# The last eight heads of the last batch divided tile by tile on chip, and finished rows stored through GpSimd's queue, in a two-layer state-space, attention and expert kernel

## The chip, the cores and the metric

The kernel runs on one core of one Trainium2 chip. The metric is the device time of the whole program in microseconds (us), taken as the median of several runs. Beside these runs there is one profiled execution, whose trace gives the durations of single instructions. All data are 32-bit floats.

## The reference

Two layers run over x of 8 x 512 rows of 256 columns. Layer 0 adds a state-space block and a top-1 expert block to x; layer 1 adds an attention block and a capacity-limited top-2 expert block. The change touches the end of layer 1 alone:

```python
xn = _layernorm(x, axis=-1)
x = x + attention(xn) + experts(xn)

q = xn @ Wq
latent_kv = (xn @ Wk + xn @ Wv) @ W_down_kv
k, v = latent_kv @ W_up_k, latent_kv @ W_up_v
scores = clip(einsum('bhqd,bhkd->bhqk', q, k) / 16)
scores = clip(scores * decay)
attn = softmax(scores, axis=-1)
out = einsum('bhqk,bhkd->bhqd', attn, v)
return out.transpose(0, 2, 1, 3).reshape(B, S, 256) @ Wo
```

There are 8 batches (b), 16 heads of 16 columns, and 512 queries and keys per batch. The softmax's division by the row sum may stand after the product with v, since the sum belongs to a query row and a head: this is what the kernel does. Each row's sum comes out of the same product, because v carries a 17th column of ones per head.

## The kernel before, in words

**Layer 1's attention.** The 16 heads of a batch are handled four at a time (group g = 0 to 3), and the 512 query rows 128 at a time (tile c = 0 to 3). One (b, g, c) is a step; there are N = 128 steps, in that order. A step has a first part (`scores`, L1370): TensorE makes `s_ps`, 128 queries by 512 keys for each of four heads; VectorE clamps it (L1382), multiplies it by the decay band and takes the row's maximum (L1384), and negates the maximum (`ng`, L1388). ScalarE then takes the exponentials (L1392). TensorE turns them (`p_ps`, L1399: four 128x128 transposes per head), ScalarE copies them out (`pT`, L1400), and TensorE multiplies with v (`values`, L1408) into `o_ps`: 32 rows per head (16 columns of v, the sum in row 16, and unused rows), four heads one above the other, 512 queries along the columns. The product is made for two tiles c at a time, columns 0 to 255 after c = 1 and 256 to 511 after c = 3.

**Dividing.** When a group's `o_ps` is full, `divide` (L1414) copies it to `os` (ScalarE, L1418) and stores it in DRAM scratch `od` (L1419). After an odd group, eight heads are read back (L1429), laid out as `oT`: head by head 16 rows, so that 128 partitions hold half of the 256 output columns. The sums come back as `sm`, 128x32 (L1430). VectorE takes the reciprocal (L1435), this goes to scratch `rd` (L1436) and comes back broadcast to 16 rows a head as `rb` (L1438); VectorE multiplies (L1441). These pieces are separated by `yield`s: in each step of the loop every waiting chain is taken one piece further. After group 3, `finish` (L1337) multiplies the turned heads with Wo (`fin`, L1341), copies this out (`fo`, L1343) and adds it to the batch's rows of `x_sb` (L1345), one tile of 128 rows at a time.

**The experts' part.** Expert outputs are added row by row into `x1` in DRAM by GpSimd's indirect DMAs (L1267). When the last one has landed, `combine` (L1354) issues on GpSimd's queue one DMA of 512 KB per batch that adds `x1`'s rows into `x_sb` (L1357). When a batch has both been added and finished, `send` (L1351) stores its 512 KB to the output from SyncE's queue (L1352).

**What sets the order.** This part is written in an order made by hand (`manual_schedule`): the program's order is every engine's order, and SyncE, GpSimd and the compute engines each work through their own list, with waits on semaphores. The loop runs over n = 0 to N + 2. In pass n it issues the scores of step n, a piece of each chain, the exponentials of step n - 1, and the transposes of step m = n - 2; when m is even, the product with v for steps m - 2 and m - 1 comes ahead of the transposes. `fill` puts pieces of the experts' work, the next batch's projections and `finish` between them; `more` takes `combine` further. After the loop the remaining chains are emptied. In SyncE's list the six stores of batches 0 to 5 stand between the two scratch stores L1419 of batch 6's groups 2 and 3.

Of the kernel before, what the change touches and what calls it, by code (L numbers as in the profile page):

```python
# [9 lines left out]
FP = mybir.dt.float32  # L10
I32 = mybir.dt.int32
AF = mybir.ActivationFunctionType
ALU = mybir.AluOpType
# [4 lines left out]
P = 128  # L18
B, S, DM = 8, 512, 256
NT = B * S  # L20
NTILE = NT // P
TPB = S // P
KC = DM // P
# [20 lines left out]
AH, AD, DL = 16, 16, 64  # L44
# [9 lines left out]
def bc(ap, axis, shape):  # L54

    return ap.unsqueeze(axis).to_broadcast(shape)
# [3 lines left out]
def tile_kernel(ctx: ExitStack, tc: tile.TileContext, t, out: bass.AP):  # L60
    nc = tc.nc
    V, A, G, T, Y = nc.vector, nc.scalar, nc.gpsimd, nc.tensor, nc.sync
# [13 lines left out]
    ident = ctile("ident", [P, P])  # L76
# [38 lines left out]
    def rows_of(src, b):  # L115
        return src[b * S : (b + 1) * S, :].rearrange("(c p) d -> p c d", p=P)
# [199 lines left out]
    for d in range(2):  # L316
        for q in range(2):
            r = slice(q * HP2, (q + 1) * HP2)
# [171 lines left out]
    with ExitStack() as es:  # L490
        p1, p2, psum = m1, m2, mp
# [22 lines left out]
        held = {}  # L514
# [206 lines left out]
        class Batch:  # L721
            def __init__(self, b):
                self.b = b
# [279 lines left out]
        N = len(chunk)  # L1003
# [35 lines left out]
        with tc.manual_schedule(engines=ENGINES):  # L1039
# [32 lines left out]
            rows, rest = itertools.chain(route0(), blocks()), late()  # L1072

            def fill(n):
                for _ in range(n):
                    if next(rows, "end") == "end":
                        next(rest, None)
# [69 lines left out]
    x_sb = res.tile([P, NTILE, DM], FP, name="x_sb", tag="x_sb")  # L1147
    with tc.tile_pool(name="a1", bufs=1) as p1, tc.tile_pool(name="a2", bufs=2) as p2, tc.tile_pool(
        name="ap", bufs=1, space=PSUM
# [139 lines left out]
        def load_some(k):  # L1289
            for to, of in loads[:k]:  # L1290
                Y.dma_start(out=to, in_=of)
            del loads[:k]
# [38 lines left out]
        def turn(pool, i):  # L1331
# [2 lines left out]
            V.tensor_copy(at, slot1[:, i, :])  # L1334
            return at

        def finish(b, oT):  # L1337
            for c in range(TPB):
                fp = bank("fin", [P, DM])
                for j in range(KC):  # L1340
                    T.matmul(fp, oT[:, j, c * P : (c + 1) * P], w_o[:, j, :], start=(j == 0), stop=(j == KC - 1))  # L1341
                fo = p2.tile([P, DM], FP, name="fo", tag="fo")
                A.copy(fo, fp)  # L1343
                xi = x_sb[:, b * TPB + c, :]
                V.tensor_tensor(xi, xi, fo, ALU.add)  # L1345
                yield
            finished.add(b)
            if b in combined:
                send(b)

        def send(b):  # L1351
            Y.dma_start(out=rows_of(out, b), in_=x_sb[:, b * TPB : (b + 1) * TPB, :])  # L1352

        def combine():  # L1354

            for b in range(B):
                G.dma_start(out=x_sb[:, b * TPB : (b + 1) * TPB, :], in_=rows_of(x1, b), accum_op=ALU.add)  # L1357
                combined.add(b)
                if b in finished:
                    send(b)  # L1360
                yield

# [49 lines left out]
        def divide(b, g, op, od, rd, held):  # L1414


            os = p1.tile([P, S], FP, name="os", tag="row", bufs=2)
            A.copy(os, op)  # L1418
            Y.dma_start(out=od[g].rearrange("i r s -> (i r) s"), in_=os)  # L1419
            yield  # L1420
            if g % 2 == 0:
                return
            j = g // 2
            if j == 0:
                held.append(p1.tile([P, KC, S], FP, name="oT", tag="oT"))
            oT = held[0]
            sm = p2.tile([P, 32], FP, name="sm", tag="sm")
            for gg in range(2):
                Y.dma_start(out=oT[64 * gg : 64 * gg + 64, j, :], in_=od[2 * j + gg, :, :AD, :])  # L1429
                Y.dma_start(  # L1430
                    out=sm[64 * gg : 64 * gg + 64, :],
                    in_=od[2 * j + gg, :, AD, :].rearrange("i (p f) -> i p f", f=32),
                )
            yield
            V.reciprocal(sm, sm)  # L1435
            Y.dma_start(out=rd[8 * j : 8 * j + 8, :].rearrange("h (p f) -> (h p) f", f=32), in_=sm)  # L1436
            rb = p1.tile([P, S], FP, name="rb", tag="row", bufs=2)
            Y.dma_start(out=rb, in_=bc(rd[8 * j : 8 * j + 8, :], 1, [8, AD, S]))  # L1438
            yield
            yield  # L1440
            V.tensor_tensor(oT[:, j, :], oT[:, j, :], rb, ALU.mult)  # L1441
            yield
            if g == 3:
                urgent.insert(0, finish(b, oT))
# [4 lines left out]
        with tc.manual_schedule(engines=ENGINES):  # L1449
# [3 lines left out]
            finished, combined = set(), set()  # L1453
            urgent, idle, chains = [], [], []
# [30 lines left out]
            def follow():  # L1485

                nonlocal work, ready, e1, e2
                if late_left:
                    last_rows(LATE[n])
                    return  # L1490
                if next(routing, "end") != "end":
                    return
                for _ in range(2):
                    if next(sends, "end") == "end" and ready is None:
                        ready = n
                        r1s.close()
                        e1 = es.enter_context(tc.tile_pool(name="f1", bufs=1, side="right"))
                        e2 = es.enter_context(tc.tile_pool(name="f2", bufs=2, side="right"))
                        work = experts()
                        next(work)  # L1500

            steps = [(b, g, c) for b in range(B) for g in range(4) for c in range(TPB)]
            N = len(steps)
            last_rows(1)
            done = []
            pT, op, pair = {}, {}, None
            inputs = {0: got}
            for n in range(N + 3):

                if n < N:  # L1510
                    b, g, c = steps[n]
                    if (g, c) == (0, 3) and b + 1 < B:
                        xT = p2.tile([P, KC, S], FP, name="xT", tag="xT")
                        Y.dma_start(out=xT, in_=xtd1[b + 1])
                    if (g, c) == (1, 2) and b + 1 < B:
                        inputs[b + 1] = {"q": [], "k": []}
                        urgent.append(inputs_of(b + 1, xT, inputs[b + 1]))
                    if (g, c) == (0, 0):
                        od = dram.tile([4, 4, 32, S], FP, name="od", tag="od", bufs=2)
                        rd = dram.tile([AH, S], FP, name="rd", tag="rd", bufs=2)  # L1520
                        scratch = (od, rd, [])
                    now = Step(b, g, c, inputs[b])
                    now.scratch = scratch
                    done.append(now)
                    now.scores()
                load_some(6)
                for chain in list(chains):
                    if next(chain, "end") == "end":
                        chains.remove(chain)
                if ready is not None and n == ready + 3:  # L1530
                    idle.append(work)
                begun = n >= 1
                if begun:
                    fill()
                if 1 <= n <= N:
                    done[n - 1].exps((0, 1))
                m = n - 2
                if m >= 0 and m % 2 == 0 and m >= 2:

                    s = done[m - 1]  # L1540
                    if s.c == 1:
                        s_op = psum.tile([P, S], FP, name="o_ps", tag="o_ps", bufs=1)
                    s.values(s_pT, s_op)
                    if s.c == TPB - 1:
                        chains.append(divide(s.b, s.g, s_op, *s.scratch))
                        next(chains[-1])
                    if begun:
                        fill()
                if 0 <= m < N:
                    if m % 2 == 0:  # L1550
                        s_pT = [p2.tile([P, TPB, 2 * P], FP, name="pT", tag="pT", bufs=5) for _ in range(4)]
                    done[m].transpose(s_pT, (0, 1))
                if begun:
                    fill() or more()
                if 1 <= n <= N:
                    done[n - 1].exps((2,))
                if 0 <= m < N:
                    done[m].transpose(s_pT, (2,))
                    if m % 2 == 1 and n < N // 2:
                        fill()  # L1560
                    done[m].transpose(s_pT, (3,))
                if begun:
                    fill() or more()
                if 1 <= n <= N:
                    done[n - 1].exps((3,))
                follow()
            while fill() or chains:
                for chain in list(chains):
                    if next(chain, "end") == "end":
                        chains.remove(chain)  # L1570
# [76 lines left out]
```

## Time and profile before

| what | value |
|---|---|
| median of the runs | 2120.34 us (three runs, 2119.49 to 2121.51) |
| the profiled execution's own time | 2089.04 us |
| its span, first to last instruction | 2087.3 us |
| mean granted TensorE clock | 0.940 of full speed |
| TensorE matmuls busy | 1838.5 us (88%) |
| VectorE busy | 1434.2 us (69%) |
| ScalarE busy | 1176.7 us (56%) |
| GpSimd busy | 624.6 us (30%) |
| SyncE's DMA queue (q1) | 116,400 packets, 137.07 MB, 20.9% of 16 engines |
| GpSimd's DMA queue (q0) | 27,504 packets, 107.25 MB, 16.8% of 16 engines |

The busy shares are means over the whole program, which has very different stages; they do not tell what the end of it waits for. For this the trace is read by place. The chain that ended last goes back from the last instruction, at each step to what released it. The timeline of one engine lists its instructions in order: start, duration, the instruction with the tiles that it writes and reads, how many of the kind were merged into the line, and in brackets the idle time ahead of it with what ended it. "SPq" lines are DMA issues on SyncE's queue; a merged line's duration reaches from its first issue to the end of its last. The windows view gives for a stretch its length, each engine's busy time with the number of instructions (TensorE, weight loads, VectorE, ScalarE, GpSimd), the granted TensorE clock, the DMA engines' busy share and GB/s. In the trace a transpose leaves one TensorE record and a matmul with data in 32 bits two, so that a `fin` tile, which is two matmuls, shows as x4.

### The profile page before, as it was taken

The numbers are of one execution on the slowest core, as the hardware profiler recorded it, in microseconds if no ns is written. First come the engines' busy times: TensorE is split into PE (matmuls) and PEld (weight loads), VectorE is DVE, ScalarE is ACT, GpSimd is POOL, SyncE is SP. The second block draws the span as 40 slices with busy tenths as digits, with TensorE's granted clock in tenths as the row PEclk, the third lists the DMA queues.
The fourth block names the chain that finished last, engine by engine and source line by source line (L and its number), as shares of the span: only waits on it lengthen the run. The fifth ranks groups of instructions, "written<-read, shape, count | busy, mean of one in ns | idle before, by whom it ended". The sixth has DMA issues, their size and how long they took to land. (4 is left out here: it accounts for less than half of the span.)

```text
span 2087.3 us, 33144 instructions
## 1 busy us (share of the span) xinstructions
PE 1838.5 (88%) x11672; PEld 1219.8 (58%) x11672; DVE 1434.2 (69%) x3299; ACT 1176.7 (56%) x2545; POOL 624.6 (30%) x565
## 2 busy tenths in 40 slices
PE   5666999999999999978776888999999999999875
PEld 5333776676677676744544445656656566665543
DVE  5684757666486756678657898766666777777783
ACT  2243454535444453545434677767677777777864
POOL 0048645446464544545420065000100000010200
PEclk9887999999999999998876889999999999999988
DMA  7113654655465565444433142231322223221711
GB/s 262 61 51 115 224 191 160 206 176 196 147 198 185 163 202 180 144 139 126 152 111 101 61 151 67 82 106 46 84 83 63 73 66 97 60 84 59 151 48 37
DMA packets 153542, 256.10 MB, mean 123 GB/s; under 512 B 23737, under 2 KB 111980, under 8 KB 141472
## 3 DMA queue, kind: packets, MB, share of 16 engines
q1 hardware_dynamic: 116400, 137.07, 20.9%
q0 software_dynamic: 27504, 107.25, 16.8%
q10 hardware_dynamic: 9472, 9.67, 1.4%
q8 instruction: 92, 1.51, 0.3%
q14 instruction: 74, 0.61, 0.1%
HBM read 185.28 MB, written 73.63 MB: 124 GB/s over the span
## 5 line engine op out<-in xcount | busy, mean ns | idle before, releaser
L1382 DVE TENSOR_SCALAR s<-s_ps 128x512 f32<-128x512 f32 x512 | 317.6, 682 | 199.9 <-PE s_ps L1377 156.4
L1392 ACT ACTIVATE s<-s,ng 128x512 f32<-128x512 f32 x512 | 355.2, 727 | 37.6 <-DVE ng L1388 37.4
L1399 PE MATMUL p_ps<-ident,s 128*128 128x128 f32 x2048 | 286.1, 283 | 48.8 <-ACT pT L1400 48.8
L1384 DVE CUSTOM_DVE_ANT_0 s<-s,band 128x512 f32<-128x512 f32 x512 | 322.9, 686 | 0.0
L1399 PEld LDWEIGHTS p_ps<-ident,s 128*128 128x128 f32 x2048 | 236.5, 144 | 128.3 <-ACT pT L1400 86.0
L1400 ACT COPY pT<-p_ps 128x512 f32<-128x512 f32 x512 | 276.6, 590 | 54.6 <-PE p_ps L1399 50.8
L1267 POOL DMA_INDIRECT x<-e_yo,e_to x28 | 44.6, 1592 | 601.1 <-ACT e_yo L1266 540.5
L732 PE MATMUL pj<-xT,w_in 128*128 128x512 f32 x384 | 204.1, 658 | 16.2 <-DVE cv L745 14.2
L1377 PE MATMUL s_ps<-kT,qT 16*128 16x512 f32 x1024 | 164.0, 671 | 27.5 <-DVE s L1382 21.0
L544 PEld LDWEIGHTS h_ps<-xdT,w 128*128 128x128 f32 x1248 | 150.1, 194 | 21.4 <-issue 20.8
L544 PE MATMUL h_ps<-xdT,w 128*128 128x128 f32 x1248 | 153.8, 277 | 1.9 <-DMA w<-in_w_dram,w_idx 1.9
L745 DVE SCALAR_TENSOR_TENSOR cv<-pj,w_conv_w,cv 128x511 f32<-128x511 f32 (+2 forms) x192 | 143.1, 746 | 10.9 <-ACT cv L741 6.9
L562 PE MATMUL y_ps<-w,hT 128*128 128x256 f32 x624 | 150.0, 385 | 0.0
L908 POOL TENSOR_TENSOR au<-da,half 128x512 f32<-128x512 f32 x64 | 76.9, 1202 | 223.0 <-PE seg L924 121.1
L562 PEld LDWEIGHTS y_ps<-w,hT 128*128 128x128 f32 x624 | 118.3, 194 | 32.5 <-issue 17.9
L1408 PE MATMUL o_ps<-pT,vt 128*32 128x256 f32 x2048 | 136.8, 408 | 0.0
L732 PEld LDWEIGHTS pj<-xT,w_in 128*128 128x128 f32 x384 | 72.6, 207 | 101.1 <-issue 93.1
L982 POOL TENSOR_TENSOR yT<-yT,ex 128x512 f32<-128x512 f32 (+1 forms) x48 | 59.1, 1231 | 221.5 <-DVE ex L981 163.4
L1248 PE MATMUL e_hp<-e_xdT,e_w 128*128 128x256 f32 x448 | 121.8, 394 | 3.1 <-ACT e_xdT L1233 2.3
L1261 PE MATMUL e_yp<-e_w,e_hT 128*128 128x256 f32 x448 | 120.1, 391 | 0.2
L937 ACT ACTIVATE mt<-seg,mid 64x64 f32<-64x64 f32 x512 | 109.5, 309 | 0.8
L1408 PEld LDWEIGHTS o_ps<-pT,vt 128*32 128x32 f32 x2048 | 64.0, 116 | 75.4 <-issue 45.2
(278 smaller groups left out, 3008.6 us busy)
## 6 DMA issues: line engine op xcount, KB each, us to landing
ex<-exd SPq DMA_DIRECT2D x96, 128.0 KB
u<-in_u_dram SPq DMA_DIRECT2D x16, 512.0 KB
xtd<-xT SPq DMA_DIRECT2D x16, 512.0 KB
fr<-fdd SPq DMA_DIRECT2D x64, 128.0 KB
od<-os SPq DMA_DIRECT2D x32, 256.0 KB
xT<-xtd SPq DMA_DIRECT2D x15, 512.0 KB
e_w<-in_ei_dram SPq DMA_DIRECT2D x7, 1024.0 KB
e_w<-in_eo_dram SPq DMA_DIRECT2D x7, 1024.0 KB
```

Of the source, the lines that this page charges most:

```text
L544: T.matmul(hp[:, i, :], w1[:, k * FF + f * P : k * FF + (f + 1) * P], xdT[:, k * P : (k + 1) * P], start=(k == 0), stop=(k == KC - 1),)
L562: T.matmul(yp, hT[f // 4][:, f % 4, :], w2[:, f * DM : (f + 1) * DM], start=(f == 0), stop=(f == FC - 1))
L732: T.matmul(pj, w_in[:, k, o * P : (o + 1) * P], self.xT[:, k, :], start=(k == 0), stop=(k == KC - 1))
L745: V.scalar_tensor_tensor(cv[:, s:], pj[:, : S - s], conv_w[:, q, 3 - s : 4 - s], cv[:, s:], ALU.mult, ALU.add)
L1248: T.matmul(hp, w1[:, k, f * P : (f + 1) * P], xdT[:, k, :], start=(k == 0), stop=(k == KC - 1))
L1377: T.matmul(sp[i], self.q[r, cols], self.k[r, :], start=True, stop=True)
L1382: V.tensor_scalar(self.p[i], sp[i], -CLAMP, CLAMP, ALU.max, ALU.min)
L1384: V.tensor_tensor_reduce(out=self.p[i], in0=self.p[i], in1=band[:, at : at + S], scale=1.0, scalar=-3.0e38, op0=ALU.mult, op1=ALU.max, acc ...
L1392: A.activation(self.p[i], self.p[i], AF.Exp, bias=self.ng[:, i : i + 1])
L1399: T.transpose(pp[:, k, :], self.p[i][:, k * P : (k + 1) * P], ident)
L1400: A.copy(pT[i][:, :, cc * P : (cc + 1) * P], pp)
L1408: T.matmul(op[32 * i : 32 * i + 32, half * 2 * P : (half + 1) * 2 * P], self.v[:, k, h * (AD + 1) : h * (AD + 1) + 32], pT[i][:, k, :], st ...
```

## The change

It has two parts.

**The last eight heads.** In batch 7, group 2's `os` is kept on chip and not stored. For group 3, `divide` is not used. A new class `Ending` handles one tile of 128 query rows: `out` copies the tile's 128 columns of `o_ps` to `osq` (ScalarE); `divide` turns group 2's and group 3's 128x128 pieces (two transposes into `tq`), so that queries are on the partitions and each head's sum is a column, takes the reciprocal of the eight sums (128x8) and multiplies (VectorE, into `oq`, 128x128); `back` turns the result (`tb`) and ScalarE copies it into `oT`; `project` multiplies with Wo (`finq`), adds to `x_sb` straight out of PSUM, and stores the tile's 128 KB from SyncE. For tiles 0 and 1 `out` and `divide` stand at the end of pass n = N, and `back` in pass N + 1 ahead of the transposes of step 127. After the loop come, in this order, `out` of tiles 2 and 3, `project` of tiles 0 and 1, and `divide`, `back` and `project` of tiles 2 and 3.

**The stores.** `send` issues on GpSimd's queue instead of SyncE's, and `combine` issues all eight loads in one piece and the stores of the finished batches in the next. In the instruction order GpSimd's list ends with eight loads and then seven stores (batches 0 to 6); SyncE's list has no 512 KB store left, and ends with four of 128 KB.

```diff
@@ -1334,6 +1334,40 @@
             V.tensor_copy(at, slot1[:, i, :])
             return at
 
+        class Ending:
+            def __init__(self, b, c, op, held):
+                self.i, self.c, self.op, (self.oT, self.os) = b * TPB + c, c, op, held
+                self.at = slice(c * P, (c + 1) * P)
+
+            def out(self):
+                self.last = p2.tile([P, P], FP, name="osq", tag="osq")
+                A.copy(self.last, self.op[:, self.at])
+
+            def divide(self):
+                tq = psum.tile([P, 2, P], FP, name="tq", tag="s_ps", bufs=4)
+                T.transpose(tq[:, 0, :], self.os[:, self.at], ident)
+                T.transpose(tq[:, 1, :], self.last, ident)
+                tq = tq.rearrange("p g (i r) -> p (g i) r", r=32)
+                sm = p2.tile([P, 8], FP, name="smq", tag="smq")
+                V.reciprocal(sm, tq[:, :, AD])
+                self.oq = p2.tile([P, 8, AD], FP, name="oq", tag="oq")
+                V.tensor_tensor(self.oq, tq[:, :, :AD], bc(sm, 2, [P, 8, AD]), ALU.mult)
+
+            def back(self):
+                tp = psum.tile([P, P], FP, name="tb", tag="s_ps", bufs=4)
+                T.transpose(tp, self.oq.rearrange("p h d -> p (h d)"), ident)
+                A.copy(self.oT[:, 1, self.at], tp)
+
+            def project(self):
+                fp = psum.tile([P, DM], FP, name="finq", tag="s_ps", bufs=4)
+                for j in range(KC):
+                    T.matmul(fp, self.oT[:, j, self.at], w_o[:, j, :], start=(j == 0), stop=(j == KC - 1))
+                V.tensor_tensor(x_sb[:, self.i, :], x_sb[:, self.i, :], fp, ALU.add)
+                Y.dma_start(out=out[self.i * P : (self.i + 1) * P, :], in_=x_sb[:, self.i, :])
+
         def finish(b, oT):
             for c in range(TPB):
                 fp = bank("fin", [P, DM])
@@ -1349,16 +1383,16 @@
                 send(b)
 
         def send(b):
-            Y.dma_start(out=rows_of(out, b), in_=x_sb[:, b * TPB : (b + 1) * TPB, :])
+            G.dma_start(out=rows_of(out, b), in_=x_sb[:, b * TPB : (b + 1) * TPB, :])
 
         def combine():
 
             for b in range(B):
                 G.dma_start(out=x_sb[:, b * TPB : (b + 1) * TPB, :], in_=rows_of(x1, b), accum_op=ALU.add)
                 combined.add(b)
-                if b in finished:
-                    send(b)
-                yield
+            yield
+            for b in finished:
+                send(b)
 
 
 
@@ -1416,6 +1450,9 @@
 
             os = p1.tile([P, S], FP, name="os", tag="row", bufs=2)
             A.copy(os, op)
+            if b == B - 1 and g == 2:
+                held.append(os)
+                return
             Y.dma_start(out=od[g].rearrange("i r s -> (i r) s"), in_=os)
             yield
             if g % 2 == 0:
@@ -1503,7 +1540,7 @@
             N = len(steps)
             last_rows(1)
             done = []
-            pT, op, pair = {}, {}, None
+            tails = []
             inputs = {0: got}
             for n in range(N + 3):
 
@@ -1524,6 +1561,9 @@
                     done.append(now)
                     now.scores()
                 load_some(6)
+                if n == N + 1:
+                    for one in tails:
+                        one.back()
                 for chain in list(chains):
                     if next(chain, "end") == "end":
                         chains.remove(chain)
@@ -1541,9 +1581,11 @@
                     if s.c == 1:
                         s_op = psum.tile([P, S], FP, name="o_ps", tag="o_ps", bufs=1)
                     s.values(s_pT, s_op)
-                    if s.c == TPB - 1:
+                    if m > N - TPB:
+                        tails += [Ending(s.b, c, s_op, s.scratch[2]) for c in (s.c - 1, s.c)]
+                    elif s.c == TPB - 1:
                         chains.append(divide(s.b, s.g, s_op, *s.scratch))
-                        next(chains[-1])
+                        next(chains[-1], None)
                     if begun:
                         fill()
                 if 0 <= m < N:
@@ -1564,6 +1606,20 @@
                 if 1 <= n <= N:
                     done[n - 1].exps((3,))
                 follow()
+                if n == N:
+                    for one in tails:
+                        one.out()
+                    for one in tails:
+                        one.divide()
+            for _ in rows:
+                pass
+            for one in tails[2:]:
+                one.out()
+            for one in tails[:2]:
+                one.project()
+            for part in ("divide", "back", "project"):
+                for one in tails[2:]:
+                    getattr(one, part)()
             while fill() or chains:
                 for chain in list(chains):
                     if next(chain, "end") == "end":
```

## The prediction

> **What bounds the kernel now.** Times are us from the span's start. I read first the chain that ended last, then the timelines of SyncE's queue and of VectorE where the chain leaves the engines for a DMA, then the stretches' clock and DMA share. Up to 1973 the chain runs through TensorE, ScalarE and VectorE, and VectorE repeats a step of one row tile every 5.05 us (its clamps start at 1963.17, 1968.21, 1973.26). It leaves the engines twice: for `od<-os` at 1975.95, and for everything after 2061.4.
>
> First place. SyncE's queue:
>
> ```profile
> 1955.99 19.87 SPq L1352 DMA_DIRECT2D out_dram<-x_sb  x6
> 1975.95 0.54 SPq L1419 DMA_DIRECT2D od<-os  x1
> ...
> 1986.39 0.51 SPq L1429 DMA_DIRECT2D oT<-od  x1
> 1986.94 0.51 SPq L1430 DMA_DIRECT2D sm<-od  x1
> ```
>
> and VectorE:
>
> ```profile
> 1978.22 0.17 DVE L1388 TENSOR_SCALAR ng<-mx 128x4 f32<-128x4 f32 x1
> 1990.53 0.35 DVE L1435 RECIPROCAL sm<-sm 128x32 f32<-128x32 f32 x1 [12.14 <-DMA sm<-od]
> 1990.80 2.42 DVE L1382 TENSOR_SCALAR s<-s_ps 128x512 f32<-128x512 f32 x4
> ```
>
> Six stores (batches 0 to 5), each waiting for its accumulating load to land, hold SyncE for 20 us. `os` was copied by 1965.09 (ACT L1418), but its store to scratch leaves at 1975.95, 10.9 us late, and lands 10.37 us later by the chain, where the same transfer takes 1.99 us on idle queues (2062.01). The reciprocal of the sums stands in VectorE's order at 1978.4, waits 12.14 us, and all scores wait behind it. The stretches:
>
> ```profile
> 1972.00:1980.00 8.00, 6.53 (x68) 3.81 (x64) 6.32 (x18) 7.01 (x13) 0.00 (x0) 1.00 1.18 239
> 1984.00:1988.00 4.00, 0.00 (x0) 0.00 (x0) 0.00 (x0) 0.00 (x0) 0.00 (x0) 0.63 0.25 86
> 1992.00:1996.00 4.00, 4.00 (x16) 1.89 (x18) 3.96 (x13) 0.10 (x1) 0.00 (x0) 0.50 0.18 66
> ```
>
> The DMA engines are full (share 1.18) from 1952 to about 1983; then all engines are empty, and TensorE comes back at clock 0.50.
>
> Second place, the tail, in the chain:
>
> ```profile
> 2058.77 2.60 PE o_ps L1408 x32
> 2062.01 1.99 DMA od<-os
> 2064.62 3.96 DMA sm<-od
> 2069.06 1.41 DMA rd<-sm
> 2070.49 3.44 DMA rb<-rd
> 2074.05 0.70 DVE oT L1441
> 2074.80 1.24 PE fin L1341 x2
> 2076.48 2.09 PE fin L1341 x4
> 2079.01 1.92 PE fin L1341 x4
> 2081.38 1.15 PE fin L1341 x4
> ```
>
> From the end of `o_ps` (2061.36) to the span's end (2087.3) are 25.9 us: a trip through DRAM to divide (12.7 to 2074.05), the multiply, projections of 8.6 us at half clock, a store of 512 KB from 2083.41 (3.9).
>
> [...]`od<-os`, in SyncE's ring behind stores, took 10.37 us. [...] Trace: last matmul at 1981.4, 0.63 in 1984 to 1988, then 0.50; eight `s_ps` take 3.86 us instead of 1.14. [...]
>
> **The change, part by part.** The sum is made against the profiled execution, 2089.04 us with a span of 2087.3; the runs' median is 2120.34, 31.3 above it, and I carry the difference in us over to it.
>
> *Stores on GpSimd.* Seven stores of 512 KB leave SyncE and stand behind the eight loads on GpSimd. Each waits there for its own load, the seventh also for VectorE's last `fin` add of batch 6. Behind them GpSimd has nothing, and only the program's end waits for them. Loads cost GpSimd 10.39 us for eight to issue, 1.3 each; I price a store the same and, as they hang on landings, up to 11.1 (the loads' median to landing): 7 x 11.1 = 78 from 1960 gives 2038, ahead of the end. Cost nothing; cover gone if a store takes 14 us.
>
> *The stall.* SyncE now issues `od<-os` at about 1965.1. The loads landed 3.1 to 3.2 us apart until stores mixed in (1955.99, 1959.10, 1962.30) and 4.4 afterwards, so all eight last until about 1956 + 7 x 3.15 = 1978; the stores follow them in one ring. The scratch store has only GpSimd's ring against it: with equal turns its 1.99 us become 3 to 4, landing at 1969. The two DMAs after it (`oT`, `sm`) and landing took 4.1 us at 1986.39; contended I take 6: 1975, 3 us before the reciprocal's place. So the 12.14 us go. Bounds: none left, or, if equal turns do not hold and the 10.37 stays, sums at 1965.1 + 10.4 + 6 = 1981.5, 3 us left; if also `sm` crawls, 6. What is late next: `rd` and `rb` (1.41 + 3.44, issued at 1978.8) have until the multiply two steps later, 10.1 us; doubled, they are in time. With no idle TensorE stays warm, and the 0.95 us that VectorE then waited for `s_ps` (before 2002.49) goes: **-13.1**.
>
> *Scratch for the last eight heads.* For g = 2 of batch 7 `os` is only held: one DMA less, hidden, 0. For g = 3 the copy of 128x512 and the whole trip go (below).
>
> *The block between steps 126 and 127.* It stands in ScalarE's order after the last exponential and before the four `pT` copies of step 127, and in TensorE's before its 16 transposes, so both wait in it, and `o_ps` and all of the ending wait for them. Now:
>
> ```profile
> 2056.35 0.75 ACT L1392 ACTIVATE s<-s,ng 128x512 f32<-128x512 f32 x1
> 2056.98 1.09 ACT L1400 COPY pT<-p_ps 128x512 f32<-128x512 f32 x2
> 2058.32 1.07 ACT L1400 COPY pT<-p_ps 128x512 f32<-128x512 f32 x2 [0.26 <-PE p_ps L1399]
> ```
>
> New prices: a 128x128 copy on ScalarE is, along 128x256 (0.37) and 128x512 (0.58), 0.27[...]; VectorE's 128x128 multiply, along 0.42 and 0.69, 0.29[...]; the reciprocal of 128x8 lies between 0.17 (128x4) and 0.35 (128x32), taken 0.2; a transpose is 0.14 in a row and 0.28 alone; the hop between engines is 0.04 to 0.06. Strided PSUM reads aren't in the trace[...]. First `osq` 2056.98 to 2057.25, transpose to 2057.6, reciprocal and multiply to 2058.2, the second tile's to 2058.75, second `tb` to 2059.1. The transposes of step 127 start at 2058.95 instead of 2056.05; from there ScalarE needs 0.65 to the first copy and 0.48 for each next: last `pT` done at 2062.05 instead of 2059.39. `o_ps` ends 1.97 later as before: 2064.05. **+2.7**; with doubled reads +4, at least +2.
>
> *The ending.* From the end of `o_ps`: two `finq` tiles of the finished columns (warm 1.03 each) 2.1; four transposes to 2.65 (their `osq` copies are done at 0.6); VectorE, after its second add (2.5), reciprocals and multiplies to 3.05 and 3.6; `tb` to 3.95; `oT` copies to 4.25; `finq` of the last two from 3.8 to 4.85 and 5.85; add to 6.35; SyncE's store. Four stores of 128 KB replace one of 512; three are under way earlier. The last is priced at `od<-os`'s 1.99 (256 KB), bounds 1.5 and 3.9. Sum 8.4 instead of 25.9: **-17.5**.
>
> *Clock.* The block leaves TensorE mostly waiting for about 2 us. At half clock `o_ps` costs 3.5 instead of 1.93 (seen at 2029.6) and each `finq` 1 more: 2.5 to 4 on the path. I allow **+1.4**.
>
> Sum: -13.1 + 2.7 - 17.5 + 1.4 = -26.5; the profiled execution would become 2062.5, the median 2093.8. Its own range: -29 (no clock loss, short store) to -19 (6 us of stall left, doubled reads), 2091 to 2101.
>
> **Rivals.** *A: the DMA engines stay the bound (0.17).* The stall came from full engines, not from the queue's order: GpSimd's ring holds loads and stores until about 1989, and the sums still land at 1985 to 1990. For: share 1.18, and no bytes go. Against: [...]the loads' own pace. Saving 26.5 less 7 to 13: 2101 to 2107.
>
> *B: the block and a cold TensorE eat half of the tail (0.10).* Strided reads at double price (+1.5), half clock from `o_ps` to the last `finq` (+4), last store 3.9 (+2): saving 19, 2101. Against: clock 1.00 from 2036 to 2064.
>
> *C: slower (0.02).* GpSimd's stores end the program. [...] If every store takes over 18 us, seven from 1960 end after 2087, and from there each us per store costs 7; at 20 us, 2133 in the median. Against: eight loads issued at 1.3 us beside a full VectorE.
>
> *D: nothing moves (0.02).* In the instruction orders of the two kernels the stores do leave SyncE and VectorE's tail is new, so only an equal loss could hide it: 2120.
>
> **How the numbers follow.** The forecast has 0.69, A 0.17, B 0.10, C 0.02, D 0.02. Range 2090 to 2106: it leaves out a little on both sides. A measurement of this kernel tells about 0.2% (4 us) from no change. Faster is the forecast with A and B, 0.96; same D, 0.02; slower C, 0.02.
>
> **What would show it.** VectorE waits under 1 us for batch 6's second reciprocal of sums, and TensorE's clock stays 1.0 there; `od<-os` at about 1965 lands within 4 us. TensorE starts step 127's transposes about 3 us after those of step 126 end. From the end of `o_ps` to the span's end 8 to 10 us; span about 2061. GpSimd's last store leaves well before. Wrong if the sums still land after 1981, or if one of the new small operations takes over 0.6 us.

## The result, and the profile after

The changed kernel takes 2100.49 us (median of seven runs, 2097.25 to 2113.6) against 2120.55 before (seven runs): ratio 0.990, interval [0.987, 0.993], 20 us less by the medians. The forecast was 2093.8, range 2090 to 2106: right in sign and range, and 7 us too good.

The profiled execution after took 2100.49 us (span 2098.8), but the one shown of before took 2089.04, 31 us under its own runs. That gap arises upstream, around 1200 to 1340 us, where GpSimd's sends of rows (L1315) wait for one line of VectorE (L1322) 50 us in the trace of after and 20 in that of before. The change is not what makes it: e5, the changed kernel on another chip, has 23.5 there. What does make it stays open. So traces are compared here by place, from the start of GpSimd's first accumulating load, which I call zero: 1949.52 before, 1979.51 after.

**The stall.** The chain of waits of after, and VectorE's timeline:

```profile
1997.92 0.59 ACT os L1452
...
1998.53 9.22 DMA od<-os
...
2008.34 7.26 DMA sm<-od
```

```profile
2015.72 0.35 DVE L1472 RECIPROCAL sm<-sm 128x32 f32<-128x32 f32 x1 [4.07 <-DMA sm<-od]
```

The stores are no longer ahead of `od<-os`: it leaves when `os` is copied (1998.5). Yet it takes 9.22 us, barely less than the 10.37 of before, and `sm` 7.26. VectorE's wait fell from 12.14 to 4.07 and did not go.

**GpSimd** carries the stores, at 0.75 us each from the third on (its timeline):

```profile
1979.51 10.46 POOL L1391 DMA_DIRECT2D x_sb<-x  x8 [2.59 <-DMA x<-e_yo,e_to]
...
2000.94 0.75 POOL L1386 DMA_DIRECT2D out_dram<-x_sb  x1 [1.90 <-DMA x_sb<-x]
2041.43 0.75 POOL L1386 DMA_DIRECT2D out_dram<-x_sb  x1 [39.74 <-issue]
```

**The ending**, from the chain:

```profile
2081.80 0.17 ACT osq L1347
...
2082.97 0.91 PE tb L1361 x2
2083.88 3.11 PE p_ps L1433 x16
2086.99 2.62 PE o_ps L1442 x32
2089.61 1.94 PE finq L1367 x8
...
2093.26 1.74 PE finq L1367 x8
```

There is no DMA left in it but the last store: 9.2 us from the end of `o_ps` to the span's end (25.9 before). No new operation is dear. The block's `osq` and `tb` stand ahead of step 127's transposes, as forecast.

**The clock** of after, in stretches (TensorE's granted clock is the third number from the end):

```profile
1988.00:1992.00 4.00, 2.10 (x14) 1.70 (x12) 4.00 (x10) 3.36 (x7) 3.50 (x4) 0.86 1.23 188
1992.00:1996.00 4.00, 4.00 (x30) 1.39 (x32) 2.76 (x8) 2.51 (x5) 1.10 (x2) 0.50 1.23 195
2016.00:2020.00 4.00, 3.33 (x8) 1.37 (x8) 4.00 (x10) 0.18 (x1) 0.00 (x0) 0.77 0.17 52
```

TensorE ran at half clock from about 1990.9 to 1997.7 with work before it; just ahead, up to 1990.56, was a gap of 1.90 us in that work. The reciprocal's place came 3.2 us later after zero than before; that the half clock did this is likely and not shown apart, but in e5, without half clock there, the place is where it was before.

### The profile page after: what moved, and what is told of

The parts are those of the page before. It is cut to its first block, busy times and chain, and to the rows that moved or that the text cites. A ratio compares the mean times of both kernels' runs of the same rounds, so it can differ in the third digit from the quotient of the medians.

```text
span 2098.8 us, 33158 instructions
## 1 busy us (share of the span) xinstructions
PE 1857.0 (88%) x11684; PEld 1227.0 (58%) x11684; DVE 1433.7 (68%) x3305; ACT 1178.8 (56%) x2548; POOL 629.1 (30%) x572
## 5 line engine op out<-in xcount | busy, mean ns | idle before, releaser
L1433 PE MATMUL p_ps<-ident,s 128*128 128x128 f32 x2048 | 296.8, 289 | 57.8 <-ACT pT L1434 49.8
L1433 PEld LDWEIGHTS p_ps<-ident,s 128*128 128x128 f32 x2048 | 245.3, 148 | 141.5 <-ACT pT L1434 84.8
L1411 PE MATMUL s_ps<-kT,qT 16*128 16x512 f32 x1024 | 167.3, 685 | 19.1 <-DVE s L1416 12.4
L544 PEld LDWEIGHTS h_ps<-xdT,w 128*128 128x128 f32 x1248 | 149.2, 192 | 22.4 <-issue 21.6
```

What stands on the lines that cost most here:

```text
L544: T.matmul(hp[:, i, :], w1[:, k * FF + f * P : k * FF + (f + 1) * P], xdT[:, k * P : (k + 1) * P], start=(k == 0), stop=(k == KC - 1),)
L1411: T.matmul(sp[i], self.q[r, cols], self.k[r, :], start=True, stop=True)
L1433: T.transpose(pp[:, k, :], self.p[i][:, k * P : (k + 1) * P], ident)
```

## The experiments

Theory: the gain is the sum of two separate parts, the ending and the order in SyncE's queue; what is left of the stall comes from GpSimd's own transfers, loads that hold back `od` and stores that hold back `sm`. Rivals: the ending gives all; the DMA engines' bytes decide, not the order; SyncE's sequencer is late. e1 to e4 ran on one chip, e5 to e8 on a second, e9 to e11 on a third, each set beside runs of the kernel before, whose medians were 2087.2 to 2087.9 us.

**e1, the kernel before once more** (no edit).

> The kernel before, unchanged, profiled once more. Why: its first profiled execution took 2089 us where its runs take 2119 to 2134, and GpSimd's eight loads began 30 us earlier in it (1949.5 us) than in the changed kernel's (1979.5). If that gap is the program's own slow or quick passage through the row-sending stage, as I think, the loads begin at about 1980 here, the execution takes about 2120, and from the first load to the end of the span it is again about 138 us, with VectorE's wait for sm at 10 to 14 us. The rival, that the change itself delays the loads by 30 us: they begin at 1950 again and the execution takes 2090.

Measured: 2088.65 us, loads from 1948.6, wait 12.43 us, 138.3 from zero to the span's end. My guess on the 31 us fell: on the chips of these experiments the kernel's medians lie near 2087, and 2120 belongs to the first timing; whether to its chip or its occasion was not tried. The rival falls too: e5 shows no delay of the loads by the change. Single profiles of the experiments start their loads anywhere from 1942 to 1952 (e8, which holds them back, apart), so stretches are counted from zero.

**e2, the new ending alone.** From the changed kernel:

```diff
 def send(b):
-    G.dma_start(out=rows_of(out, b), in_=...)
+    Y.dma_start(out=rows_of(out, b), in_=...)
...
     combined.add(b)
-yield
-for b in finished:
-    send(b)
+    if b in finished:
+        send(b)
+    yield
```

> The new ending alone (tile by tile, divided by columns and turned back); the six finished batches' stores stay on SyncE's queue as before the change. My theory, that the two halves are separate sums: 13 us less than before (about 2107), with VectorE's wait for sm still near 12 us and 17 to 18 us from the last exponential to the end of the span. Rival one, the ending gives all of it: 20 us less (about 2100). Rival two, the ending takes effect only when the queue is cleared: 5 us less or none.

Measured: 2069.76 against 2087.16, ratio 0.992 [0.990, 0.993], 17.4 us less, between my 13 and the first rival's 20. VectorE still waits 12.1 us for `sm`; from the last exponential to the span's end 17.3 us instead of e1's 32.2. The ending's gain is its own, and by place it is 15; the profile's loads also began 3 us earlier than e1's.

**e3, the stores' move alone** (the kernel before, with the edits of e2 the other way and batch 7's store left on SyncE).

> The stores' move alone: the old ending, with the last batch's own store left on SyncE so that the end is the same; batches 0 to 6 are stored through GpSimd's queue behind the eight loads. My theory: VectorE's wait for sm falls from 12 us to about 4, the stretch from the last exponential to the end stays near 31 us, and the whole is 5 to 8 us less than before (2112 to 2115). Rival, the stores' move is worth all that I forecast for it: 13 us less (2107). Rival two, it is worth nothing, since the DMA engines carry the same bytes: 2119 to 2121.

Measured: 2078.83, ratio 0.996 [0.994, 0.997], 8.3 us less; the stretch from the last exponential to the end stays at 31.0. Waits of VectorE from the first load on, e3:

```profile
DVE sm L1435 <- DMA sm<-od: 21.8, 2, 16.3
```

Two waits, the longer one (16.3) in the old ending; batch 6's is 5.45, where I expected about 4. The bytes have stayed and 7 of 12.4 us have gone, so the order does matter; but the move isn't worth the 13 of my sum. 17.4 and 8.3 make 25.7, for 22.8 measured of both together (e5), within the intervals. By place, from zero to the span's end, the parts are 15.2 and 7.2, together 22.4, and both at once 21.2.

**e4 and e6, the six stores on SyncE but late** (from the changed kernel; `send` on SyncE):

```diff
     for b in range(B):
         G.dma_start(out=x_sb[...], in_=rows_of(x1, b), accum_op=ALU.add)
         combined.add(b)
     yield
-    for b in finished:
-        send(b)
...
     Y.dma_start(out=rb, in_=bc(rd[8 * j : 8 * j + 8, :], 1, [8, AD, S]))
+    if b == B - 2 and g == 3:
+        for f in sorted(finished):
+            send(f)
```

> The changed kernel, with the six stores back on SyncE's queue but placed behind the whole of batch 6's second trip to DRAM (after rb), so that od, oT, sm, rd and rb go ahead of them. GpSimd's queue then holds the eight loads alone. If it is the order in a queue that matters and not whose queue it is, VectorE's wait for sm is gone or as small as in the changed kernel. If loads waiting in GpSimd's ring hold back the first packet of od by 4 us, od still takes 5 to 7 us from issue to landing, but sm then takes 2 to 3 instead of 7.3, and the wait of 4.07 goes: about 4 us less than the changed kernel, 2095 to 2097. If the stores hold od back, it lands within 3 us. If neither, the wait stays at 4 and the time at 2100.

> The stores on SyncE's queue behind batch 6's second trip, once more, so that it is compared with the changed kernel on one chip. If what it gained over the changed kernel is real (30.4 us less than before against 20.8, on two chips): 6 to 10 us less than the changed kernel here, of which 4 to 5.5 are the wait for sm and the rest is TensorE's clock, which no longer falls behind that wait. Rival, a difference of chips: only the 4 to 5 us of the wait.

**e5, the changed kernel on e6's chip** (no edit).

> The changed kernel, unchanged, beside the next three on one chip. From the parts measured alone (the ending 17.4 us, the stores' move 8.3), if the parts add: 20 to 27 us less than before. VectorE's wait for sm is 4 to 5.5 us, and od takes 7.5 to 9.5 us from issue to landing.

Measured: e4 2056.74, ratio 0.985 [0.984, 0.987]. e5 2065.13 (2063.32 to 2066.96), 0.989 [0.988, 0.991]; e6 2059.30 (2056.62 to 2062.97), 0.987 [0.985, 0.988]. On one chip the late stores gain 5.8 us over the changed kernel, and no run of e6 is as slow as the fastest of e5. That is about the wait, 6.38 us in e5 (I expected 4 to 5.5) and none in e6; a gain of clock on top, which I had added, is not seen. VectorE in e5, then in e6:

```profile
1979.65 0.35 DVE L1472 RECIPROCAL sm<-sm 128x32 f32<-128x32 f32 x1 [6.38 <-DMA sm<-od]
```

```profile
1976.46 0.35 DVE L1470 RECIPROCAL sm<-sm 128x32 f32<-128x32 f32 x1
```

SyncE's timeline in e5, then in e6:

```profile
1960.01 0.32 SPq L1456 DMA_DIRECT2D od<-os  x1
...
1968.77 0.51 SPq L1466 DMA_DIRECT2D oT<-od  x1
1969.33 0.51 SPq L1467 DMA_DIRECT2D sm<-od  x1
1980.04 0.32 SPq L1473 DMA_DIRECT2D rd<-sm  x1
```

```profile
1963.22 0.32 SPq L1454 DMA_DIRECT2D od<-os  x1
...
1972.09 0.51 SPq L1464 DMA_DIRECT2D oT<-od  x1
1972.65 0.51 SPq L1465 DMA_DIRECT2D sm<-od  x1
1976.84 0.32 SPq L1471 DMA_DIRECT2D rd<-sm  x1
```

The second `oT` waits for `od`, so its issue shows the landing: 8.8 and 8.9 us, stores or not (8.9 in e4, where I had expected 5 to 7). With e8 below, the loads alone do this. From `sm`'s issue to `rd` it is 10.7 us with the stores beside it and at most 4.2 without: the stores do that. DMA packets of e5 in 1961 to 1963, then in 1965 to 1966 (q0 is GpSimd's queue, q1 SyncE's; packets, MB, share of 16 engines):

```profile
q0 software_dynamic: 392, 0.40, 123.8%
```

```profile
q0 software_dynamic: 117, 0.12, 73.7%
q1 hardware_dynamic: 69, 0.14, 41.8%
```

The first packet of `od` goes 4.3 us after its issue (up to 1964.8 four of its packets, against 870 of GpSimd's from 1960.4 on); then it gets its turns.

**e7, the late stores through GpSimd** (e4's places; `send` on GpSimd, held by a copy):

```diff
+    G.tensor_copy(p2.tile([P, 1], FP, name="gate", tag="gate"), rb[:, :1])
     for f in sorted(finished):
         send(f)
```

> As the one before, but the six late stores go through GpSimd's queue: a one-column copy of rb on GpSimd holds them until rb has landed. If only the place of the stores in time matters and not whose queue carries them, this is equal to the kernel with the stores late on SyncE within 0.2%, sm lands within 4 us of its issue and the wait is gone. If GpSimd's queue costs something of its own, it is 2 us or more slower.

Measured: 2059.96, 0.986 [0.985, 0.988], no wait for `sm`. That is within 0.7 us of e6, as expected: for these stores it is of no weight whose queue carries them, only when they run.

**e8, the loads late too** (the changed kernel; the same copy ahead of the eight loads, batches 6 and 7 first).

> The changed kernel, with the eight loads themselves, and so the stores behind them, held back by a one-column copy of rb on GpSimd until rb has landed; batches 6 and 7 are loaded first. Nothing then moves beside od and sm. If the loads are what holds od back: od lands about 2 us after its issue instead of 9, sm within 3, the wait is gone, and the time is that of the kernel with late stores within 0.3%. If od takes its 9 us even so, the cause is not GpSimd's transfers. If the load of batch 6 is then late for the adds of its rows, VectorE waits there by a few us and the time is 2 to 8 us longer.

Measured: 2060.09, 0.986 [0.985, 0.988]. SyncE's timeline:

```profile
1960.26 0.32 SPq L1456 DMA_DIRECT2D od<-os  x1
...
1962.28 0.51 SPq L1466 DMA_DIRECT2D oT<-od  x1
```

With nothing beside it `od` lands in 2.0 us, its first packets 0.8 after the issue. The wait at batch 6 is gone, and there is none at the adds; 1.0 us comes back at batch 7, whose own trip now meets the delayed stores.

**e9, one load at a time** (e4, with a copy behind each load that reads its rows):

```diff
     G.dma_start(out=x_sb[...], in_=rows_of(x1, b), accum_op=ALU.add)
+    G.tensor_copy(p2.tile([P, 1], FP, name="gate", tag="gate"), x_sb[:, b * TPB, :1])
```

> The kernel with the stores late on SyncE's queue, and after each of the eight loads a one-column copy on GpSimd that reads the rows just loaded, so that a load is issued only when the one before has landed and never more than one stands in GpSimd's ring. If it is the depth of loads already waiting that keeps od's first packet back for 4 to 5 us, od starts within 1 to 2 us here and lands 3 to 6 us after its issue instead of 8.5. If one running load is enough to hold it back, od still takes 8 to 9 us. Nothing waits for sm in either case, so the time is that of the kernel with late stores, unless the adds of batch 6's rows or the stores now wait for the slower loads: then up to 10 us more.

Measured: 2069.04, 0.991 [0.989, 0.993]; nearly 10 us more than e6 on another chip, of which 9.4 are a wait of VectorE's add for my copy. `od`, issued at 1963.0, sends its first packet at 1965.7 and lands at 1967.7, in 4.7 us. Packets of 1964 to 1965, then of 1966 to 1967:

```profile
q0 software_dynamic: 184, 0.19, 118.1%
```

```profile
q1 hardware_dynamic: 141, 0.26, 73.9%
q0 software_dynamic: 36, 0.03, 17.6%
```

One running load holds it back for 2.7 us, until that load is nearly through (I expected 1 to 2); a row of loads for 4.3. The next load is issued at 1968.3, so nothing of it stands beside the rest of `od`.

**e10, `od` issued by ScalarE** (the changed kernel):

```diff
-    Y.dma_start(out=od[g].rearrange("i r s -> (i r) s"), in_=os)
+    (A if (b, g) == (B - 2, 3) else Y).dma_start(out=od[g].rearrange("i r s -> (i r) s"), in_=os)
```

> The changed kernel with one DMA issued elsewhere: batch 6's last od goes out from ScalarE's queue instead of SyncE's, behind the copy that makes it. If the delay lies in the DMA engines, where loads stand ahead of it, od still takes 8 to 9.5 us to land and the time is the changed kernel's within 0.3%. If SyncE's own ring or sequencer was late, od lands 4 us sooner and the wait for sm of 4 to 6 us shrinks by as much.

Measured: 2063.44, 0.988 [0.986, 0.990], wait 5.75 us. On its own queue `od` still takes 7.6 us (1965.72 to 1973.36), with none of its packets up to 1970 and the first 12 in 1970 to 1971, 4.3 to 5.3 us after the issue. SyncE's own queue and sequencer are not the cause.

**e11, the ending undivided** (e4, all four tiles after the last values):

```diff
-for one in tails[2:]:
-    one.out()
-for one in tails[:2]:
-    one.project()
-for part in ("divide", "back", "project"):
-    for one in tails[2:]:
+for part in ("out", "divide", "back", "project"):
+    for one in tails:
         getattr(one, part)()
```

with the calls inside the loop taken out.

> The kernel with late stores, with the first two tiles of the ending no longer divided between steps 126 and 127: all four are copied out, divided, turned back, multiplied and stored after the last values. By my sum the block costs 2.7 us where it stands; taking it out brings the last values 2.5 us earlier, and the second pair of tiles then has the first pair's work ahead of it: two osq (0.9 us), four transposes and two turns back, and four more products (about 1.0), on ScalarE, VectorE and TensorE in turn, 2 to 4 us. So within 0.1% of the kernel with late stores, 2 us either way. If the block is what costs and the rest overlaps: 2 to 3 us faster. If the ending is bound by its serial steps: 3 us slower.

Measured: 2056.07, 0.985 [0.983, 0.987]. From the last exponential to the end of `o_ps` 5.0 us instead of 7.5, from there to the span's end 10.2 instead of 8.9 (e6): 1.2 less in all by the traces, too little to tell by the times across chips. This version and e6 beat both kernels, by 31.6 and 28.6 us against the kernel before.

## Why the prediction was right in sign and 7 us too good

The number stayed in its range, but the mechanism of its second largest term was half wrong, and the signs that I had named for it say so: VectorE waits 4 to 6 us and not under 1, `od` lands after 8.8 (9.2 in the first trace) and not within 4, and the sums land 35.1 us after zero in e5, which is 1984.6 on the scale of before. "Wrong if the sums still land after 1981" has come true. That the range held is not luck alone: its lower bound of the gain counts 6 us of stall left. The stretches, each from its profile (us; "slot" is where the reciprocal of batch 6's second sums could have started, "exp" the start of step 127's last exponential; sums are taken before rounding):

| stretch | before | after | e1 (before) | e5 (after) | e6 | forecast of the difference | e5 less e1 |
|---|---|---|---|---|---|---|---|
| zero to slot | 28.9 | 32.1 | 28.8 | 28.7 | 28.8 | 0 | 0 |
| wait for `sm` | 12.1 | 4.1 | 12.4 | 6.4 | 0 | -12.1 | -6.0 |
| reciprocal to exp | 65.8 | 65.3 | 64.9 | 65.3 | 64.8 | -1.0 | +0.4 |
| exp to end of `o_ps` | 5.0 | 8.6 | 5.0 | 7.5 | 7.5 | +2.7 | +2.5 |
| end of `o_ps` to end | 25.9 | 9.2 | 27.2 | 9.2 | 8.9 | -17.5 | -18.0 |
| clock allowance | | | | | | +1.4 | in the rows above |
| sum | 137.8 | 119.3 | 138.3 | 117.1 | 110.1 | -26.5 | -21.2 |

- *Stores on GpSimd cost nothing*: right for the issue (0.75 us each) and for the end (the last at 2041). What they do to `sm` belongs to the next term.
- *The stall, -13.1*: here it failed. "The scratch store has only GpSimd's ring against it: with equal turns its 1.99 us become 3 to 4." The issue was right (15.5 us after zero in e5, 15.6 forecast) and so was the slot; the landing was not: 8.8 us. The turns were assumed from the first moment. Two streams that were both running did share equally (in 1976 to 1978 of before, 242 packets of GpSimd's and 238 of SyncE's), but `od` got its first turn after 4.3 us (e5), after 0.8 with no loads (e8), and on another queue it fared the same (4.3 to 5.3, e10). The prediction also read the 10.37 us of before as the work of the order in SyncE's queue; with nothing ahead in that queue `od` still takes 8.8. What the order had cost was the late issue, 10.9 us. Then `sm`, priced at 6 with what goes before it, met the stores and by the chain took 10.2 in e5 (e6: no wait). The bound "if also `sm` crawls, 6" was nearly the measured 6.4; I had both ends and took the wrong one.
- Rival A comes nearest (7 to 13 lost, 2101 to 2107, sums at 1985 to 1990), and half of its cause holds: GpSimd's traffic does delay the sums. But the queue's order was a cause too, worth 7 us of the wait (e3), and the engines need not stay the bound: e6 moves the same bytes and has no wait. It is what has been issued ahead of a transfer, and when.
- *TensorE stays warm, -1.0*: not got. After the 6.4 us of waiting the clock falls as before (0.50 in e5 from 1980). Without the wait there is no clear gain either: e6 has 64.8 in this row, against 64.9 and 65.8 in the two traces of before. Half-clock stretches with TensorE at work, as at 1992 in the first trace of after, were not foreseen. One also comes in before, from 2029.4 to 2032.8, 2.0 us after a gap of 1.28 us in TensorE's work; one in e6, where the 0.57 of the window from 1980 stands for 3.4 us at half clock; and in e5 the `o_ps` at 2028.72 takes 3.34 us by the chain (3.38 in e6's stretch), where it took 1.93 at 1967.22. In after it lasts 6.7 us. A gap of 1.36 in before (ahead of 1960.10) had none after it (1.00 from 1960 to 1984), so the gap alone is not the cause, which stays open. The windows view of e6, where TensorE had no long wait:

```profile
1980.00:1984.00 4.00, 4.00 (x40) 1.39 (x32) 3.96 (x11) 2.35 (x4) 0.00 (x0) 0.57 1.00 312
```

- *The block, +2.7*: 2.5. *The ending, 8.4 left*: 9.2. What was too small is the last store: from the end of the last add to the span's end are 3.3 us in e5, where 1.99 was taken and 3.9 was the bound; the rest came 0.5 sooner. The new prices were right: `osq` 0.27, reciprocal of 128x8 0.20, multiply 0.29, `finq` 0.99 for a tile. *Clock allowance, +1.4*: not needed in e5 (1.00 to the end); it was needed in the first trace, at step 127's transposes (0.69 in 2084 to 2088).

That turns begin at once was my estimate; no trace of before showed it. In e5, from 1960.4 to 1964.8, 870 of GpSimd's packets went, about 1 KB each (0.86 MB), and only four of `od`'s. By my estimate from these, that is 54 to each of the 16 DMA engines, if they are spread evenly. Where they stood ahead of `od`, no run here tells.

## What to carry to other kernels

Taking large transfers out of the queue of a small one removes the delay of its issue, here worth 7 us of a stall of 12.4, and only that: large transfers already running on another queue still held its first packet back by 4.3 us. What protected the small transfer further was when the large ones were issued, not whose queue they used. Price such a transfer as start plus turns (for `od` 4.3 and 4.5 us in e5, 0.8 and 1.2 alone in e8), and take the pessimistic bound while loads are in flight. If its result is due soon, issue the bulk after it: here that was worth another 6 us. And a round trip through DRAM to divide at the very end of this program was dearer than some thirty small operations on chip: an ending of 25.9 us against 9.2, with 2.5 more for the block ahead of it.

## What the runs showed of the hardware

- A 256 KB store issued beside a row of 512 KB accumulating loads: first packet after 4.3 us (e5), 2.7 with one load running (e9), 0.8 alone (e8); landing after 8.8, 4.7 and 2.0 us. Over the eight traces with a row of loads it landed after 7.4 (e11) to 9.2 us (after).
- The loads land 2.63 us apart once all are issued and no other transfer runs (after: stores released at 1993.03, 1995.66, 1998.29, and between them packets of the loads alone), not the 3.1 to 3.2 that I read from before, where GpSimd was still issuing loads up to 1959.9.
- TensorE's granted clock was half with TensorE at work for 3.4 us in before (2029.4 to 2032.8) and in e6 (0.57 in 1980 to 1984), and for 6.7 us in after (1990.9 to 1997.7); what brings this on is open.
- The kernel before takes 2120 us in the first timing and 2087 on the three chips of the experiments, with the same ratio of the changed kernel to it within the intervals (0.990 and 0.989).
